# A fixed table for the ends of blocks in a four-layer sparse graph attention kernel: 18 finer steps, each half moved by itself

## The chip, the core and the metric

The kernel runs on one core of one Trainium2 chip. The metric is the device time of one execution in microseconds (us), lower is better. Three runs of the kernel before took 2247.27, 2250.97 and 2253.18 us; their median is 2250.97 us.

A core has engines that each run their own instructions in order: TensorE (PE, matrix products; its weight loads are shown apart as PEld), VectorE (DVE), ScalarE (ACT) and GpSimd (POOL). SP is the queue from which plain transfers (DMA) are issued; indirect gathers are issued by POOL.

## The reference

A batch of 16 graphs shares one adjacency matrix of 1024 nodes (about 8 neighbours a node). Four layers follow each other; layers 0, 2 and 3 are attention layers, layer 1 is a graph attention layer of one head.

```python
Q, K, V = (h @ Wq), (h @ Wk), (h @ Wv)            # 8 heads of 16
scores = einsum('bnhd,bmhd->bhnm', Q, K) / sqrt(16)
attn = softmax(where(adj == 0, -inf, scores))      # over the neighbours
x = layer_norm(h + einsum(attn, V) @ Wo + bo)
y = relu(x @ W1 + b1) @ W2 + b2                    # 128 -> 256 -> 128
x = layer_norm(x + y)
# layer 1: z = x @ W; scores = leaky_relu(z @ a_src + (z @ a_dst)^T), masked, softmax;
#          x = layer_norm(attn @ z + x)
```

Everything is in 32-bit floats[...].

## The kernel before, in words

**Tiling.** The 16 graphs are cut into two groups `g` of 8. The nodes are sorted by degree and dealt into 8 blocks `t` of 128. A *block* (called unit `u` in the code) is one layer, one group, 128 nodes: 16 blocks to a layer, 64 in all. The neighbours of a block are fetched from a table of keys and values in HBM, by indirect gathers; each block has some 4 to 6 *parts* of two gathered neighbours a partition (usually five: P0, P1, P2, then MIX, a part of one neighbour, then P4).

**One iteration of the main loop is one part** (lines 1160 to 1219). For an attention block DVE multiplies the gathered keys with the queries (`products`, L958), sums over the head dimension (L981), ACT takes the exponential (L985), DVE multiplies the gathered values with it one iteration later (`weighted`, L1009), and PE adds the rows up with a 0/1 matrix into PSUM (`summed`, `acc`, L1025). Products live in four buffers `pr`; a fifth one waits until PE has summed the oldest. P0 and P1 are summed together, in the iteration of MIX. POOL then issues the gathers of the part four ahead into the buffer that was just read.

**The end of a block.** When all parts are summed, the reciprocal of the denominators is taken (`divided`, L1062), and two *halves* of four graphs each (`h` = 0 and 1, here a and b) get their tile `o` (L1065) and a generator `attention_tail` (L703). The tail does everything else of the layer: transpose of `o` and the bias on the residual (L712, L717), Wo (L721, L722), layer norm (`normed`: squares L624, reciprocal root L630 and L631, scaling L639), transpose (L727), W1 and relu (L732, L741), W2 (L746, L750), layer norm, transpose, and the keys and values for the next layer's table (`project`, L576, L580, L585). In the last layer there are output transposes and an indirect store instead.

**What sets the order.** All engines follow the order of the program (`manual_schedule`). Each iteration has three *openings*, calls of `others()`: opening A after `summed`, before L981 and the exponential; opening B after the exponential, before L1009; opening C at the end of the iteration. A tail is a chain of steps (`yield`), 13 for half a; half b starts one step later. At an opening the pace is added up, and each time it reaches 1, `advance(tails)` moves both halves by one step. The pace is even: `(STEPS - LATE)` = 12 or 11 steps over the 14 openings after the first. So the last one or two steps of a block fall into the next. Every opening also takes one step of the side work: the query generator of the next block (`queries`, L880: for each half a projection and copy, L900 and L904, and then four repetitions over partitions with four copies, L909 and L912), loads, and in layer 0 the slow making of the second group's table. The first opening of a block's tail is opening C of the next block's second part; A, B and C of the parts P2, MIX and P4 follow, then A, B and C of the first part and A and B of the second part of the block after: 15 openings where a block has five parts.

**Buffers that the steps touch.** `banks`: four PSUM banks for all passing products (the four repetitions of a half of the queries take all four). `ybanks`: two. `hidden()`, the tile of relu outputs `f1`: one, shared by both halves. `o`, `oT`: two each.

Of the kernel before, what the change touches and what calls it, by code (L numbers as in the profile page):

```python
# [137 lines left out]
def sparse_path(ctx: ExitStack, tc: tile.TileContext, a: dict, out: bass.AP, flag):  # L138
# [474 lines left out]
    def normed(y, dve=False):  # L613

        z = twos.tile([P, GH, D], F32, tag="o", name="z")
        total = smalls.tile([P, GH], F32, tag="total", name="total")
        if dve:
            nc.vector.tensor_copy(z, y)
            nc.vector.tensor_tensor(z, z, y, ALU.mult)
            nc.vector.tensor_reduce(total, z, mybir.AxisListType.X, ALU.add)  # L620
            nc.vector.tensor_scalar(total, total, 1.0 / D, EPS, ALU.mult, ALU.add)
        else:
            for i in range(GH):
                nc.scalar.activation(  # L624
                    z[:, i, :], y[:, i, :], AF.Square, scale=D**-0.5, bias=root,
                    accum_out=total[:, i : i + 1],
                )
        yield
        rstd = smalls.tile([P, GH], F32, tag="rstd", name="rstd")
        nc.scalar.activation(rstd, total, AF.Ln)  # L630
        nc.scalar.activation(rstd, rstd, AF.Exp, scale=-0.5)  # L631
        if dve:
            nc.vector.tensor_tensor(
                z, y,
                rstd.rearrange("p (g o) -> p g o", o=1).to_broadcast([P, GH, D]), ALU.mult,
            )
            return z
        for i in range(GH):
            nc.scalar.activation(z[:, i, :], y[:, i, :], AF.Copy, scale=rstd[:, i : i + 1])  # L639
        return z  # L640
# [62 lines left out]
    def attention_tail(l, g, t, h, o):  # L703
        layer = LAYERS[l][0]
        p = {n: w[layer, n] for n in ATTN if (layer, n) in w}
        xt = xs[l, g, t][:, h]
        last = (l, g, t) == units[-1]
        dve = last and h > 0
        for _ in range(0 if last else h):
            yield  # L710
        oT = twos.tile([P, GH, P], F32, tag="oT", name="oT")
        turned(o, oT, dve=dve)  # L712

        if dve:
            nc.vector.tensor_scalar(xt, xt, p["bo"], None, ALU.add)
        else:
            nc.scalar.activation(xt, xt, AF.Identity, bias=p["bo"])  # L717
        yield
        ps = ybanks.tile([P, GH, D], F32, tag="yps", name="yps")
        for i in range(GH):  # L720
            nc.tensor.matmul(ps[:, i, :], oT[:, i, :], p["Wo"], start=True, stop=False)  # L721
            nc.tensor.matmul(ps[:, i, :], xt[:, i, :], centre, start=False, stop=True)  # L722
        yield
        z = yield from normed(ps, dve)
        yield
        x1 = twos.tile([P, GH, P], F32, tag="oT", name="x1")
        turned(z, x1, p["ln1_g"], p["ln1_b"], dve)  # L727
        yield
        f1 = (queries_of_shared if dve else hidden)().rearrange("p (f c) -> p f c", f=F)
        for f in range(F):  # L730
            ps = bank([P, GH * P])
            nc.tensor.matmul(  # L732
                ps, p["W1"][:, f * P : (f + 1) * P], x1.rearrange("p g n -> p (g n)"),
                start=True, stop=True,
            )
            if dve:
                nc.vector.tensor_scalar(
                    f1[:, f, :], ps, p["b1"][:, f : f + 1], 0.0, ALU.add, ALU.max
                )
            else:  # L740
                nc.scalar.activation(f1[:, f, :], ps, AF.Relu, bias=p["b1"][:, f : f + 1])  # L741
        yield
        ps = ybanks.tile([P, GH, D], F32, tag="yps", name="yps")
        for i in range(GH):
            for f in range(F):
                nc.tensor.matmul(  # L746
                    ps[:, i, :], f1[:, f, i * P : (i + 1) * P], p["W2"][:, f, :],
                    start=(f == 0), stop=False,
                )
            nc.tensor.matmul(ps[:, i, :], x1[:, i, :], centre, start=False, stop=True)  # L750
        yield
        z = yield from normed(ps, dve)
        yield
        yield from finish(l, g, t, h, z, p["ln2_g"], p["ln2_b"], dve)
# [55 lines left out]
    def at_once(g):  # L810
# [12 lines left out]
        for t in range(T):  # L823
# [9 lines left out]
            while both:  # L833
                advance(both)
                yield

    def exponents():
        return exps.tile([P, MOST * G * H], F32, tag="ex", name="ex")

# [40 lines left out]
    def queries(u):  # L880

        l, g, t = units[u]
        if not is_attention(u):
            ps = bank([P, J + 1, G])
            for j in range(J):
                nc.tensor.matmul(ps[:, j, :], rep_of(j, True), srcs[g, t], start=True, stop=True)
            for s, (j, _) in enumerate(QUARTERS[t]):
                at = slice(32 * s, 32 * s + 32)
                nc.tensor.matmul(
                    ps[at, MIX, :], rep_of(j, True)[:, at], srcs[g, t], start=True, stop=True  # L890
                )
            ofs[u] = smalls.tile([P, J + 1, G], F32, tag="of", name="of")
            nc.scalar.copy(ofs[u], ps)
            return
        qs[u] = reps.tile([P, J, ROW], F32, tag="qr", name="qr")
        for h in range(HF):
            q = ones_.tile([P, GH * D], F32, tag="q", name="q")
            ps = bank([P, GH, D])
            for i in range(GH):
                nc.tensor.matmul(  # L900
                    ps[:, i, :], xs[l, g, t][:, h, i, :], w[LAYERS[l][0], "Wq"],
                    start=True, stop=True,
                )
            nc.scalar.copy(q, ps.rearrange("p g d -> p (g d)"))  # L904
            yield
            pss = []
            for j in range(J):
                ps = bank([P, GH * D])
                nc.tensor.matmul(ps, rep_of(j), q[32 * j : 32 * j + 32], start=True, stop=True)  # L909
                pss.append(ps)  # L910
            for j in range(J):
                nc.scalar.copy(qs[u][:, j, h * GH * D : (h + 1) * GH * D], pss[j])  # L912
            yield

    def shared(u):

# [136 lines left out]
    def divided(u):  # L1053

        l, g, t = units[u]
        heads, d = (H, HD) if is_attention(u) else (1, D)
        den = bank([P, G * heads])
        for n, c in enumerate(sum(PIECES[t], [])):
            marked(t, c, den, exs[u][:, n, :])
        both = smalls.tile([P, 2, G * heads], F32, tag="both", name="both")  # L1060
        yield
        nc.vector.reciprocal(both[:, 1, :], den)  # L1062
        for h in range(HF):
            o = twos.tile([P, GH, D], F32, tag="o", name="o")
            nc.vector.tensor_tensor(  # L1065
                o.rearrange("p g (a d) -> p (g a) d", d=d),
                accums[u][:, h, :].rearrange("p (a d) -> p a d", d=d),
                both[:, 1, h * GH * heads : (h + 1) * GH * heads]
                .rearrange("p (a o) -> p a o", o=1)
                .to_broadcast([P, GH * heads, d]),  # L1070
                ALU.mult,
            )
            tails.append((attention_tail if heads > 1 else graph_tail)(l, g, t, h, o))
        nc.scalar.copy(both[:, 0, :], den)
        yield
        n = G * heads
        nc.gpsimd.tensor_tensor(seen[:, :, :n], seen[:, :, :n], both, ALU.add)
# [14 lines left out]
                free.append(gen)  # L1092

    pace = [0.0, 0.0]

    def idle():
        return slow if held[0] or not busy[0] else []

    def others():
        pace[0] += pace[1]  # L1100
        while pace[0] >= 1.0:
            advance(tails)
            pace[0] -= 1.0
        while True:
            gens = fronts or loads or idle()
            if not gens:
# [5 lines left out]
            if got == "idle":  # L1112
                advance(idle())
            break
        for _ in range(eager[0]):
            advance(idle())

    eager = [1]

    with tc.manual_schedule():  # L1120
# [39 lines left out]
        for i in range(len(parts) + 2):  # L1160
# [45 lines left out]
                    pass  # L1206
            if closing is not None and here:
                while any(gen not in free for gen in tails):
                    advance(tails)
                next(closing)  # L1210
                sizes, closing = closing, None
                passes = 3 if is_attention(u) else 4
                steps = STEPS if is_attention(done) else GRAPH_STEPS
                steps -= LATE[units[done][0]]
                pace[:] = 0.0, steps / (passes * sum(part[0] == u for part in parts) - 1)
            others()
            if i + 1 >= len(parts) or parts[i + 1][0] != u:

                while fronts:
                    advance(fronts)  # L1220
        while tails:
            advance(tails)
        for _ in closing:
# [438 lines left out]
```

## Time and profile before

| what | value |
|---|---|
| median of three runs | 2250.97 us |
| profiled execution | 2254.23 us, span 2251.9 us, TensorE clock granted 0.962 |
| PE busy | 2043.1 us, 91% |
| DVE busy | 1872.9 us, 83% |
| ACT busy | 1528.3 us, 68% |
| POOL busy | 1016.3 us, 45% |
| DMA | 636.05 MB, mean 282 GB/s |

The busy time is a union of the engine's intervals in the span. The mean of one instruction in a group is its latency, which for pipelined matmuls is longer than the distance between two of them; where the text needs a price it uses the distance in the timeline. Waits are inferred from semaphores: a row says which engine and line stood idle, for whom, how long in all, how often, and the longest.

### The profile page before, as it was taken

Reading aid. Unit: us, or ns where it says so; the run is one execution under the profiler, and the core shown is the slowest. Engines: PE = TensorE matmul, PEld = TensorE weight load, DVE = VectorE, ACT = ScalarE, POOL = GpSimd, SP = SyncE. Lnnn points to the kernel's source line nnn. Section 1 sums busy time; section 2 is a strip of 40 time slices with the busy share of each in tenths; the row PEclk is TensorE's granted clock in tenths of the full one; section 3 lists DMA queues with packets and bytes.
Section 4 is the critical chain, followed back from the end, with each engine's and each line's share of the span. In section 5 each row is a group of like instructions: output and inputs, shape, how many; then the busy total and the mean of one; then the engine's idle time right before and its main releaser. Section 6 shows DMA issues by size and latency. Waiting matters only on the chain.

```text
span 2251.9 us, 36507 instructions
## 1 busy us (share of the span) xinstructions
PE 2043.1 (91%) x13140; PEld 1271.3 (56%) x13140; DVE 1872.9 (83%) x1472; ACT 1528.3 (68%) x5041; POOL 1016.3 (45%) x699
## 2 busy tenths in 40 slices
PE   6589999899999999998999989999999998998986
PEld 5456665555555555554556655656655555555554
DVE  7897899888887577768988889989798998888893
ACT  3346777777777655555677777777777777676765
POOL 3343445354435368884343434334444544453540
PEclk8799999999999999999999999999999998999999
DMA  7897877778788699997997978887888788687860
GB/s 254 290 323 275 298 272 279 268 263 289 284 296 272 221 341 356 360 358 291 327 329 268 318 260 302 303 313 276 284 282 305 265 286 279 225 279 271 288 227 21
DMA packets 164700, 636.05 MB, mean 282 GB/s; under 512 B 34568, under 2 KB 37384, under 8 KB 116014
## 3 DMA queue, kind: packets, MB, share of 16 engines
q0 software_dynamic: 88720, 485.08, 61.0%
q1 hardware_dynamic: 75792, 148.57, 19.1%
q8 instruction: 105, 1.72, 0.3%
q14 instruction: 83, 0.68, 0.1%
HBM read 581.08 MB, written 92.34 MB: 299 GB/s over the span
## 4 chain that ended last, share of the span: by engine, by line
PE 41%; ACT 18%; issue 16%; DVE 11%; DMA 9%; POOL 5%; POOLq 0%; DVEq 0%; ACTq 0%
PE acc L1025 9%; DMA e<-table,idx 8%; PE yps L746 5%; PE ps L576 4%; POOL e L946 4%; PE ps L646 4%; ACT qr L912 4%; PE ps L732 3%; PE ps L909 3%; DVE pr L958 3%; ACT z L624 3%; DVE sc L981 3%; DVE pr L1009 2%; PE yps L750 2%; ACT z L639 2%
## 5 line engine op out<-in xcount | busy, mean ns | idle before, releaser
L946 POOL DMA_INDIRECT e<-table,idx x576 | 854.1, 1483 | 1101.8 <-DVE pr L1009 902.1
L1009 DVE TENSOR_TENSOR pr<-e,ex 128x2048 f32<-128x2048 f32 (+1 forms) x320 | 661.6, 2076 | 46.7 <-ACT ex L985 24.9
L958 DVE TENSOR_TENSOR pr<-e,qr 128x2048 f32<-128x2048 f32 x192 | 441.6, 2300 | 132.7 <-PE acc L1025 55.7
L1025 PE MATMUL acc<-pr,marks 128*32 128x512 f32 x2624 | 519.1, 608 | 14.8 <-DVE pr L1009 10.8
L981 DVE TENSOR_REDUCE sc<-pr 128x128 f32<-128x2048 f32 (+1 forms) x240 | 497.5, 2073 | 8.0
L624 ACT ACTIVATE z<-yps,root 128x128 f32<-128x128 f32 x888 | 317.5, 388 | 35.7 <-PE yps L765 17.2
L1025 PEld LDWEIGHTS acc<-pr,marks 128*32 128x32 f32 x2624 | 107.7, 110 | 269.4 <-issue 226.7
L639 ACT ACTIVATE z<-yps,rstd 128x128 f32<-128x128 f32 x888 | 254.0, 369 | 7.2
L746 PE MATMUL yps<-W,f 128*128 128x128 f32 x1520 | 251.8, 283 | 7.3 <-ACT f L741 1.8
L741 ACT ACTIVATE f<-ps,b 128x512 f32<-128x512 f32 x190 | 129.8, 695 | 157.6 <-PE ps L732 157.2
L746 PEld LDWEIGHTS yps<-W,f 128*128 128x128 f32 x1520 | 205.0, 192 | 51.0 <-issue 25.6
L576 PE MATMUL ps<-Wkv,xT 128*128 128x256 f32 x768 | 215.0, 419 | 20.0 <-ACT xT L652 16.7
L912 ACT COPY qr<-ps 128x512 f32<-128x512 f32 x384 | 197.3, 600 | 40.6 <-PE ps L909 40.5
L909 PE MATMUL ps<-q,rep 32*128 32x512 f32 x768 | 175.3, 661 | 34.7 <-ACT q L904 33.5
L732 PE MATMUL ps<-x,W 128*128 128x512 f32 x384 | 190.4, 620 | 12.5 <-ACT x L654 12.5
L624 ACT ACTIVATION_READ_ACCUMULATOR z<-yps,root 128x1 f32 x888 | 201.7, 227 | 0.0
L646 PE MATMUL ps<-ident,z 128*128 128x128 f32 x896 | 177.5, 299 | 25.5 <-ACT z L639 20.7
L646 PEld LDWEIGHTS ps<-ident,z 128*128 128x128 f32 x896 | 115.2, 142 | 149.2 <-ACT z L639 72.1
L580 ACT COPY kv<-ps 128x512 f32<-128x512 f32 x176 | 103.2, 589 | 131.9 <-PE ps L576 119.4
L576 PEld LDWEIGHTS ps<-Wkv,xT 128*128 128x128 f32 x768 | 146.5, 205 | 76.4 <-ACT xT L652 21.1
L721 PE MATMUL yps<-Wo,oT 128*128 128x128 f32 x768 | 160.3, 292 | 8.6 <-ACT oT L652 8.5
L722 PE MATMUL yps<-centre,x 128*128 128x128 f32 x768 | 155.5, 285 | 3.6
(176 smaller groups left out, 2597.7 us busy)
## 6 DMA issues: line engine op xcount, KB each, us to landing
table<-kv SPq DMA_DIRECT2D x88, 512.0 KB, 6.5
kept<-xT SPq DMA_DIRECT2D x96, 256.0 KB, 5.4
x<-kept SPq DMA_DIRECT2D x48, 512.0 KB, 9.2
qx<-qr SPq DMA_DIRECT2D x48, 256.0 KB, 6.7
e<-table,idx POOLq DMA_INDIRECT x576, 8.1
table<-kv SPq DMA_DIRECT2D x32, 256.0 KB, 7.7
qx<-qr SPq DMA_DIRECT2D x18, 384.0 KB, 9.1
qx<-qr SPq DMA_DIRECT2D x42, 128.0 KB, 8.1
```

The source lines that it names most:

```text
L576: nc.tensor.matmul(ps[:, k, :], x[:, i + k, :], w[LAYERS[l][0], "Wkv"], start=True, stop=True,)
L624: nc.scalar.activation(z[:, i, :], y[:, i, :], AF.Square, scale=D**-0.5, bias=root, accum_out=total[:, i : i + 1],)
L639: nc.scalar.activation(z[:, i, :], y[:, i, :], AF.Copy, scale=rstd[:, i : i + 1])
L646: nc.tensor.transpose(ps[:, i, :], z[:, i, :], ident)
L732: nc.tensor.matmul(ps, p["W1"][:, f * P : (f + 1) * P], x1.rearrange("p g n -> p (g n)"), start=True, stop=True,)
L746: nc.tensor.matmul(ps[:, i, :], f1[:, f, i * P : (i + 1) * P], p["W2"][:, f, :], start=(f == 0), stop=False,)
L912: nc.scalar.copy(qs[u][:, j, h * GH * D : (h + 1) * GH * D], pss[j])
L946: nc.gpsimd.indirect_dma_start(out=es[i][:, k, :], out_offset=None, in_=tables[l, g][:, :], in_offset=bass.IndirectOffsetOnAxis(ap=idx[:, ...
L958: nc.vector.tensor_tensor(prs[i][0][:, :n, :], es[i][:, :n, :ROW], qx[u].rearrange("p (o c) -> p o c", o=1) if (MIX, 0) in piece else of_p ...
L981: nc.vector.tensor_reduce(sc[:, :n, :], prs[i][0][:, :n, :].rearrange("p k (a d) -> p k a d", d=HD), mybir.AxisListType.X, ALU.add,)
L1009: nc.vector.tensor_tensor(prs[i][k0 // 2][:, :m, :].rearrange("p k (a d) -> p k a d", d=d), es[i][:, k0 : k0 + m, base : base + ROW].rearr ...
L1025: nc.tensor.matmul(outs[32 * j : 32 * j + 32], marks[:, mark, :], rhss, start=(chunk == mine[0]), stop=(chunk == mine[-1]),)
```

## The change

1. **Finer steps.** A tail has 18 steps instead of 13. `normed` yields once more, between the reciprocal root and the scaling (twice a tail); the transpose of `o` and the bias are two steps; the two halves of W1 and relu are two; W2 is two steps of two graphs. In order: 1 transpose of `o`, 2 bias, 3 Wo, 4 squares, 5 root, 6 scaling, 7 transpose, 8 and 9 W1 and relu, 10 and 11 W2, 12 squares, 13 root, 14 scaling, 15 transpose, 16 to 18 keys and values of the next layer.
2. **A table instead of the pace.** `PLAN` has one string for each of 15 openings. An `a` moves half a by one step, `b` half b, `q` takes one step of the side work. The strings hold 18 a, 18 b and 15 q. Beyond the table an opening does `abq`. The initial wait of half b (one step) is gone. The table drives the tails of attention blocks; those of layer 1 keep the pace.
3. **Queries in smaller pieces.** The repetitions of one half are two steps: the four products with the first two copies, and the last two copies. A query generator has six steps instead of four.
4. At the end of a block the drain of unfinished tails goes through the table too, and so does the rest after the last part.

```diff
+    PLAN = (
+        "aaqbabaqqb", "aqa", "qb", "a", "bbaabaqb", "abqq", "a", "baaqbb", "qqa", "", "bqqbqaaab", "", "", "q", "bbb",
+    )
@@ normed
         nc.scalar.activation(rstd, rstd, AF.Exp, scale=-0.5)
+        yield
@@ attention_tail
-        for _ in range(0 if last else h):
-            yield
         oT = twos.tile([P, GH, P], F32, tag="oT", name="oT")
         turned(o, oT, dve=dve)
-
+        yield
         if dve:
...
                 nc.scalar.activation(f1[:, f, :], ps, AF.Relu, bias=p["b1"][:, f : f + 1])
-        yield
+            yield
...
             nc.tensor.matmul(ps[:, i, :], x1[:, i, :], centre, start=False, stop=True)
-        yield
+            if i % 2:
+                yield
@@ queries
                 nc.scalar.copy(qs[u][:, j, h * GH * D : (h + 1) * GH * D], pss[j])
-            yield
+                if j % 2:
+                    yield
@@ the openings
+    def planned(beyond="abq"):
+        n = opening[0]
+        opening[0] += 1
+        for c in PLAN[n] if n < len(PLAN) else beyond:
+            if c == "q":
+                aside()
+                continue
+            for gen in tails:
+                if half_of[gen] == "ab".index(c):
+                    step(gen, tails)
+                    break
...
     def others():
+        if opening[0] is not None:
+            planned()
+            for _ in range(eager[0]):
+                advance(idle())
+            return
         pace[0] += pace[1]
         while pace[0] >= 1.0:
             advance(tails)
             pace[0] -= 1.0
+        aside()
...
                 while any(gen not in free for gen in tails):
-                    advance(tails)
+                    if opening[0] is None:
+                        advance(tails)
+                    else:
+                        planned("ab")
...
+                opening[0] = 0 if is_attention(done) else None
```

More of the change, by code (lines that the diff above doesn't have):

```diff
@@ L1073, in divided @@
             tails.append((attention_tail if heads > 1 else graph_tail)(l, g, t, h, o))
+            half_of[tails[-1]] = h
         nc.scalar.copy(both[:, 0, :], den)
@@ L1094, in sparse_path, with step @@
     pace = [0.0, 0.0]
+    opening = [None]
+    half_of = {}
+    def step(gen, gens):
+        got = next(gen, "end")
+        if got == "end":
+            gens.remove(gen)
+        elif got == "free":
+            free.append(gen)
+    def planned(beyond="abq"):
[9 more added lines that the diff above has]
+                    break
     def idle():
@@ L1103, in others, with aside @@
             pace[0] -= 1.0
+        aside()
+        for _ in range(eager[0]):
+            advance(idle())
+    def aside():
         while True:
@@ L1114, in others @@
             break
-        for _ in range(eager[0]):
-            advance(idle())
     eager = [1]
@@ L1215, in sparse_path @@
                 pace[:] = 0.0, steps / (passes * sum(part[0] == u for part in parts) - 1)
+                if is_attention(done) and opening[0] is None:
+                    for gen in list(tails):
+                        if gen in free:
+                            for _ in gen:
+                                pass
+                            tails.remove(gen)
+                opening[0] = 0 if is_attention(done) else None
             others()
@@ L1220, in sparse_path @@
                     advance(fronts)
+        while opening[0] < len(PLAN):
+            planned()
         while tails:
```

## The prediction

> **What bounds the kernel now.** I read the page first, then the busy time of one steady block, then who waits for whom in a steady stretch (1100 to 1640 us, most of layer 2), then that stretch in order of time.
>
> The page's busy line, and from the table of stretches one block of layer 2 (length, then PE, weight loads, DVE, ACT, POOL busy):
>
> ```profile
> PE 2043.1 (91%) x13140; PEld 1271.3 (56%) x13140; DVE 1872.9 (83%) x1472; ACT 1528.3 (68%) x5041; POOL 1016.3 (45%) x699
> ...
> 1524.00:1560.00 36.00, 34.32 (x224) 21.67 (x223) 32.13 (x19) 27.52 (x88) 14.18 (x10) 1.00 0.91 319
> ```
>
> In 36 us PE is busy 34.3, DVE 32.1, ACT 27.5. No engine is full; nothing has more than 9 us to give. The reciprocal L1062 marks the blocks: its starts in DVE's timeline lie 550.1 us apart over the 15 intervals of layer 2 and 540.8 over those of layer 3, 36.4 us a block. DVE's own work in a block, by the distances in its timeline (2.32 + 2.2 + 2.2 a part, 3.5 for MIX, 1.9 for reciprocal and the two `o`) is 4 x 6.72 + 3.5 + 1.9 = 32.3. So 4.1 us a block are waits of DVE. Which ones, by the view of waits of DVE from 1100 to 1640 us (total, times, longest; 14.8 blocks):
>
> ```profile
> DVE pr L958 <- PE acc L1025: 21.7, 12, 4.0
> DVE pr L958 <- DMA e<-table,idx: 19.2, 8, 5.5
> DVE pr L1009 <- ACT ex L985: 6.6, 4, 3.5
> DVE both L1062 <- PE ps L1025: 5.5, 3, 2.7
> ```
>
> A block loses 1.5 us to the product buffer that PE has not yet summed, 1.3 to a late gather, only 0.45 to a late exponential, 0.4 to the denominators. The first of them in order of time (start, length, engine):
>
> ```profile
> 1153.45 1.29 DVE L1065 TENSOR_TENSOR o<-acc,both 128x512 f32<-128x512 f32 x2
> ...
> 1163.76 2.28 DVE L1009 TENSOR_TENSOR pr<-e,ex 128x2048 f32<-128x2048 f32 x1
> 1170.09 2.29 DVE L958 TENSOR_TENSOR pr<-e,qr 128x2048 f32<-128x2048 f32 x1 [4.05 <-PE acc L1025]
> ```
>
> After `o`, DVE runs P2 and MIX without a stop and then needs the buffer of P0; PE frees it only here:
>
> ```profile
> 1164.35 1.86 PE L909 MATMUL ps<-q,rep 32*128 32x512 f32 x8
> ...
> 1168.13 1.92 PE L1025 MATMUL acc<-pr,marks 128*32 128x512 f32 x16
> ```
>
> And ACT at the same time, one queue in the order of the program, the exponential of MIX last:
>
> ```profile
> 1164.46 0.59 ACT L652 COPY oT<-ps 128x512 f32<-128x512 f32 x1 [1.63 <-PE ps L646]
> 1164.94 0.72 ACT L717 ACTIVATE x<-x,bo 128x512 f32<-128x512 f32 x1
> 1165.57 2.04 ACT L912 COPY qr<-ps 128x512 f32<-128x512 f32 x4
> 1167.46 0.41 ACT L624 ACTIVATE z<-yps,root 128x128 f32<-128x128 f32 x1
> ...
> 1168.85 0.31 ACT L985 ACTIVATE ex<-sc 128x64 f32<-128x64 f32 x1
> ```
>
> What is placed ahead of an exponential on ACT delays it; before the change little is, and MIX's exponential comes 15 us after `o` half a (1154.1).
>
> **What the skill says.** The Trainium skill, "PSUM — Partial Sum Buffer", section "Engine vs sequencer instructions", has ScalarE's and VectorE's queues as strict FIFO, and matmuls as starting and completing in program order. The trace agrees: L985 at 1168.85 follows exactly the copies and squares issued ahead of it. "Perfetto Trace Analysis", section "Optimization Strategy", says that the same bubble repeated can mean that no buffer is free for the next tile; the 1.5 us a block at L958 is such a one.
>
> **The change, part by part.** No arithmetic is added or removed: the same instructions in another order. A `yield` costs nothing on the chip. All is in what stands ahead of what.
>
> *Where the steps fall.* In layers 2 and 3 the old pace gives openings 1 to 3 of a block (counted from 0) the first three steps, the queries' rest and the old block's last steps, and opening 4 nothing. The table gives opening 0 a1 a2 q b1 a3 b2 a4 q q b3, opening 1 a5 q a6, 2 q b4, 3 a7, and opening 4 b5 b6 a8 a9 b7 a10 q b8. Openings 1, 4, 7 lie before the exponentials of P2, MIX, P4. Summing of P0 and P1 comes right before opening 4.
>
> *Ledger of ACT from `o` half a (time 0) to MIX's exponential.* Prices are distances in the timeline above and around it: copy 0.5 to 0.6, bias 0.7, four squares 1.4, root 0.45, scaling 1.1, four query copies 2.0, relu 0.7, transposed copy with gain 0.75, exponential 0.3. Opening 0: 0.5+0.7+0.6+0.5+0.7+1.4+2.0 = 6.4. Opening 1: 0.45+0.6+1.1, and the exponential of P2: 2.45. Openings 2 and 3: 1.0+1.4+0.75 = 3.15. Opening 4: 0.45+1.1+0.7+0.7+0.75+1.0+0.7 = 5.4. Together 17.4, plus what ACT must wait for: the first transpose 0.9; Wo of a 0.5; the second query projection 1.0 (queued behind b3 on PE); and the relu of b8. There is one `f1`: b8 writes it before a11, the last reader of a's, has been issued, so that relu waits for W2's second half on PE. With PE at 14.2 (below) and W1 of a twice 0.9, transpose 0.6, relus and half of W2 to 19, W1 of b 0.9, a11 1.3, it ends near 21.2: 2.0 us of wait. MIX's exponential ends at 17.4+0.9+0.5+1.0+2.0+0.3 = 22.1. Before it came at 15.
>
> *DVE in that time.* Rest of `o` 0.6, P2 with P1's weighting 6.7, MIX's two products 2.4: at 9.7 it wants the exponential of P2, which ACT has at 0.9+6.4+0.5+0.45+1.0+0.6+1.1+0.3 = 11.25: stall 1.55. Weighting to 13.5. Then P4 needs the sum of P0 and P1. PE: opening 0 0.1+0.6+1.1+0.6+2.0+1.8+2.0 = 8.2, projection 1.1, wait for its copy on ACT to 9.9, repetitions 1.8, transpose 0.6, sum 1.9: 14.2, stall 0.7. P4's two operations end at 18.7, and MIX's weighting waits to 22.1: stall 3.4. After it the table is thin (11 and 12 are empty, and the exponential of P4 is 0.3 late). Sum 32.3+1.55+0.7+3.4+0.3 = 38.25. The late gather (in these blocks the next P0's, 15 us from its weighting to landing at 1720 to 1735) gets over 16 us now and is hidden; that gain is in the sum.
>
> *What the hand count leaves out.* The same count for the old order gives 32.3 + 1.3 gather + 0.2 for `acc`, some 34 to 35, against 36.4 measured: hand-overs and bank waits of about 1.5. In the new order part of them disappear under the ACT queue. I take half, 0.75: 39.0, or 2.6 more a block. Ends for it: 0 and 1.5, so 1.85 to 3.4.
>
> *The rest.* The wait of PE for the query copy (`PE ps L909 <- ACT q L904`, 17.9 us in 14.8 blocks, 1.2 each) goes away for half a of the queries; PE then stands about 3 us at the transpose of `o` instead, which is at nothing because DVE sets the end there. If that cover were gone it would be worth up to 1.2. The last keys and values leave their block earlier, which nobody waits for: the table they fill is read 8 blocks later. The SP stores and POOL's `seen` move with them, ahead of no gather that is due. Layer 1 has one more step a tail; PE is busy 148.8 of 155 us there, the order hardly counts: bound 0 to 5 us, taken 0. The very end alternates the halves as before: -3 to 3, taken 0.
>
> *Sum.* Blocks with an attention block on both sides: 15 in layer 0, 15 in layer 2, one between layers 2 and 3, 15 in layer 3: 46. 46 x 2.6 = 120. The profiled execution of 2254.2 (span 2251.9 and 2.3 around it) becomes 2374; it lies 3.3 above the median, which becomes 2371.
>
> **Rivals.**
> *Faster.* The bubbles close: `acc` is on time (1.5 a block) and ACT keeps up. 46 x 1.5 = 69 less, 2182. It decides if MIX's exponential is done before 18.7, that is if ACT's ledger of 17.4 waited for under 1.3 us in all. For it: ACT is 24% idle, and PE's waits for ACT's copies are real. Against: 17.4 of the block's 27.5 us of ACT work stand in half of its time. Chance 0.10.
> *About the same, a little slower.* The relu of b8 waits 0, not 2, because PE is ahead: stalls 1.55+0.7+1.4+0.3, block 36.25 to 37.0, at most 46 x 0.6 = 28: 2245 to 2290. For it: the wait of b8 is nowhere in the old trace. Chance 0.16, a third of it within 0.3%.
> *Much slower.* Every hand-over counts in full and delays the next block's queries (last copy at 20 of the block, needed at 23) or the first layer's slow work: 41 a block, 46 x 4.6 = 212, 2463. Chance 0.10.
> The forecast: 0.64, its own range 2310 to 2440.
>
> **How the numbers follow.** 0.3% (7 us) is what a measurement of this kernel can tell from no change. Faster: the first rival, 0.10. Same 0.05. Slower 0.85. Cutting the faster rival, most of the much slower one and the bottom of the second leaves 2262 to 2445.
>
> **What would show it.** Right: DVE's waits for `ex` (L985) rise from 0.45 to about 5 us a block and are the largest row; the gather row nearly vanishes; blocks of 39 us; ACT f L741 waits for PE yps L746, which has no large row now; PE's share falls below 88%. Wrong: blocks under 36.4, or DVE's waits still led by `acc` and gathers. If `ex` is not late, the ledger is wrong; if ACT does not wait at b8, only its 2.0 is.

## The result and the profile after

The changed kernel takes 2380.18 us (median of 6 runs), the kernel before 2249.12 us on the same chips: a ratio of 1.0583, 95% interval 1.0553 to 1.0613, slower. The forecast was 2371, slower, range 2262 to 2445. The profiled execution is 2377.5 us, its span 2375.3.

The page of the changed kernel, its busy line, and from the table of stretches one block of layer 2 (from one reciprocal to the next):

```profile
PE 2004.4 (84%) x13140; PEld 1289.1 (54%) x13140; DVE 1875.7 (79%) x1472; ACT 1531.3 (64%) x5041; POOL 1037.2 (44%) x699
```

```profile
1567.60:1606.00 38.40, 33.61 (x220) 22.11 (x220) 32.35 (x20) 27.82 (x88) 15.16 (x10) 0.96 0.82 287
```

The work is the same, and the shares are lower because it stands in more time (the busy time of DVE and ACT is within 3 us of before, that of PE is 39 us less). DVE is busy 32.35 us of the block, against 32.13 in the block shown of the kernel before. What the block is longer, 2.4 us, is nearly all waits. The view of waits of DVE in layer 2 of the changed kernel (1141 to 1713 us; total, times, longest):

```profile
DVE pr L1014 <- ACT ex L990: 62.5, 36, 3.3
DVE pr L963 <- PE acc L1030: 10.1, 12, 1.4
DVE pr L963 <- ACT qr L916: 9.8, 2, 4.9
DVE pr L963 <- DMA qx<-qr: 4.0, 1, 4.0
```

(L963, L986, L990, L1014 are L958, L981, L985, L1009 of the kernel before.) The wait for the exponential (L990) has gone from the third row to the first; the gather's row is gone; `acc` has halved. In order of time, DVE in one block, the stalls alone:

```profile
1580.23 2.29 DVE L1014 TENSOR_TENSOR pr<-e,ex 128x2048 f32<-128x2048 f32 x1 [1.66 <-ACT ex L990]
1583.36 2.29 DVE L963 TENSOR_TENSOR pr<-e,qr 128x2048 f32<-128x2048 f32 x1 [0.83 <-PE acc L1030]
...
1590.45 1.23 DVE L1014 TENSOR_TENSOR pr<-e,ex 128x1024 f32<-128x1024 f32 x1 [2.48 <-ACT ex L990]
...
1597.06 2.29 DVE L1014 TENSOR_TENSOR pr<-e,ex 128x2048 f32<-128x2048 f32 x1 [0.86 <-ACT ex L990]
```

Four stalls: P2, the sum of P0 and P1, MIX, P4, 5.83 us together. The last three repeat almost to the hundredth from block to block (the next block has 1.46, 0.83, 2.49, 0.86). The first does not. Two other blocks of the same layer, in the view of stretches (its third number from the end is the granted clock of PE):

```profile
1528.02:1567.59 39.57, 34.67 (x220) 23.29 (x220) 32.36 (x20) 27.83 (x88) 15.15 (x10) 0.91 0.82 291
1644.19:1680.96 36.77, 32.09 (x226) 20.57 (x226) 32.35 (x19) 27.61 (x88) 18.05 (x10) 1.00 0.80 283
```

DVE and ACT are as busy in the one as in the other. In the first DVE waits 2.83 us for P2's exponential, in the second not at all. PE stands some 3 us before the transpose of `o` in both (3.13 and 3.02). After that its clock is 0.50 from 1529 to 1535 us in the first, and 1.00 in the second; one microsecond of each, with 7 and 12 matmul instructions:

```profile
1529.44 1.09 PE L647 MATMUL ps<-ident,o 128*128 128x128 f32 x4 [3.13 <-DVE o L1070]
1532.00:1533.00 1.00, 1.00 (x7) 1.00 (x6) 0.96 (x2) 0.58 (x1) 0.00 (x0) 0.50 1.00 395
1648.00:1649.00 1.00, 1.00 (x12) 1.00 (x11) 0.96 (x2) 1.00 (x2) 1.00 (x1) 1.00 1.10 363
```

So Wo comes later, and with it the squares on ACT and the exponential behind them. Nineteen blocks of five parts in layers 2 and 3 (left out are those next to a change of layer or behind a block of six parts, and one more with other work on DVE) fall in order: 36.8 us at a mean clock of 1.00 (four blocks), 38.1 to 38.4 at 0.95 to 0.96 (eight), 38.5 to 38.6 at 0.93 (three), 39.5 to 39.6 at 0.89 to 0.91 (four). In the kernel before no such order is seen; it has a block of 38.65 us at 1.00 and one of 35.62 at 0.90, and PE stands before `o` only three times in these two layers, 3.5 us in all.

And ACT ahead of MIX's exponential, with its wait for the single `f1`:

```profile
1586.82 1.06 ACT L916 COPY qr<-ps 128x512 f32<-128x512 f32 x2
1589.59 0.69 ACT L740 ACTIVATE f<-ps,b 128x512 f32<-128x512 f32 x1 [1.70 <-PE yps L745]
1590.17 0.25 ACT L990 ACTIVATE ex<-sc 128x64 f32<-128x64 f32 x1
```

`o` half a was ready at 1568.86 (L1070 from 1568.17, two of 0.69); MIX's exponential ends at 1590.42, 21.6 us later, where the ledger had 22.1.

Where the 123 us of the two spans lie, by the starts of the reciprocals number 1, 9, 16, 32, 40, 48, 56 and 64 in DVE's timeline; the last column runs from the last one to the end:

| us | start | layer 0, g 0 | layer 0, g 1 | layer 1 | layer 2, g 0 | layer 2, g 1 | layer 3, g 0 | layer 3, g 1 | end |
|---|---|---|---|---|---|---|---|---|---|
| before | 161.8 | 322.5 | 247.1 | 310.9 | 293.7 | 296.6 | 295.1 | 287.6 | 36.6 |
| changed | 164.6 | 353.4 | 266.2 | 317.3 | 301.0 | 310.6 | 313.6 | 307.1 | 41.6 |
| exponentials first | 160.5 | 318.9 | 230.1 | 312.9 | 281.2 | 283.2 | 290.8 | 279.7 | 40.5 |
| old pace, exponentials first | 166.0 | 340.2 | 266.3 | 310.6 | 299.0 | 295.6 | 292.8 | 286.2 | 38.5 |
| finer steps, old places | 162.2 | 346.1 | 228.7 | 332.0 | 280.1 | 282.7 | 294.6 | 291.3 | 48.0 |

### The profile page after: what moved, and what is told of

The parts are those of the page before. It is cut to its first block, busy times and chain, and to the rows that moved or that the text cites. A ratio compares the mean times of both kernels' runs of the same rounds, so it can differ in the third digit from the quotient of the medians.

```text
span 2375.3 us, 36561 instructions
## 1 busy us (share of the span) xinstructions
PE 2004.4 (84%) x13140; PEld 1289.1 (54%) x13140; DVE 1875.7 (79%) x1472; ACT 1531.3 (64%) x5041; POOL 1037.2 (44%) x699
## 4 chain that ended last, share of the span: by engine, by line
PE 48%; ACT 19%; DVE 17%; issue 11%; DMA 3%; POOL 2%; POOLq 0%; DVEq 0%; ACTq 0%
PE acc L1030 8%; PE yps L745 8%; ACT z L624 6%; PE ps L647 6%; DVE pr L1014 6%; PE ps L731 4%; DVE pr L963 4%; ACT z L640 4%; PE ps L904 4%; PE yps L720 4%; PE yps L721 4%; PE yps L749 4%; ACT qr L916 3%; PE ps L913 3%; PE ps L576 2%
## 5 line engine op out<-in xcount | busy, mean ns | idle before, releaser
L951 POOL DMA_INDIRECT e<-table,idx x576 | 922.4, 1601 | 1180.6 <-DVE pr L1014 950.3
L1014 DVE TENSOR_TENSOR pr<-e,ex 128x2048 f32<-128x2048 f32 (+1 forms) x320 | 660.8, 2074 | 268.8 <-ACT ex L990 243.6
L986 DVE TENSOR_REDUCE sc<-pr 128x128 f32<-128x2048 f32 (+1 forms) x240 | 497.5, 2073 | 8.1
L963 DVE TENSOR_TENSOR pr<-e,qr 128x2048 f32<-128x2048 f32 x192 | 438.8, 2286 | 69.9 <-PE acc L1030 35.3
L1030 PEld LDWEIGHTS acc<-pr,marks 128*32 128x32 f32 x2624 | 108.0, 111 | 290.8 <-issue 237.2
L745 PE MATMUL yps<-W,f 128*128 128x128 f32 x1520 | 243.0, 281 | 2.5 <-ACT f L740 1.5
L647 PE MATMUL ps<-ident,o 128*128 128x128 f32 x384 | 85.9, 367 | 171.4 <-DVE o L1070 167.3
L576 PE MATMUL ps<-Wkv,xT 128*128 128x256 f32 x768 | 204.7, 407 | 20.5 <-ACT xT L653 16.4
L916 ACT COPY qr<-ps 128x512 f32<-128x512 f32 x384 | 202.5, 604 | 13.1 <-PE ps L913 12.9
L740 ACT ACTIVATE f<-ps,b 128x512 f32<-128x512 f32 x190 | 131.0, 692 | 115.9 <-PE yps L745 82.4
L647 PE MATMUL ps<-ident,z 128*128 128x128 f32 x896 | 159.5, 291 | 47.3 <-ACT qr L916 22.3
L624 ACT ACTIVATION_READ_ACCUMULATOR z<-yps,root 128x1 f32 x888 | 188.4, 212 | 0.0
L647 PEld LDWEIGHTS ps<-ident,z 128*128 128x128 f32 x896 | 106.9, 142 | 144.4 <-ACT qr L916 50.4
L990 ACT ACTIVATE ex<-sc 128x128 f32<-128x128 f32 (+1 forms) x240 | 73.2, 307 | 165.7 <-DVE sc L986 165.6
L647 PEld LDWEIGHTS ps<-ident,o 128*128 128x128 f32 x384 | 63.1, 192 | 191.7 <-issue 136.9
```

The costliest lines, as they stand in the source:

```text
L576: nc.tensor.matmul(ps[:, k, :], x[:, i + k, :], w[LAYERS[l][0], "Wkv"], start=True, stop=True,)
L624: nc.scalar.activation(z[:, i, :], y[:, i, :], AF.Square, scale=D**-0.5, bias=root, accum_out=total[:, i : i + 1],)
L647: nc.tensor.transpose(ps[:, i, :], z[:, i, :], ident)
L745: nc.tensor.matmul(ps[:, i, :], f1[:, f, i * P : (i + 1) * P], p["W2"][:, f, :], start=(f == 0), stop=False,)
L951: nc.gpsimd.indirect_dma_start(out=es[i][:, k, :], out_offset=None, in_=tables[l, g][:, :], in_offset=bass.IndirectOffsetOnAxis(ap=idx[:, ...
L963: nc.vector.tensor_tensor(prs[i][0][:, :n, :], es[i][:, :n, :ROW], qx[u].rearrange("p (o c) -> p o c", o=1) if (MIX, 0) in piece else of_p ...
```

## The experiments

Two theories stood at the start. **Q**: the loss is the queue; exponentials stand behind tail steps on ACT. **P**: the loss is PE's, which now stands for long before the transpose of `o` and whose granted clock has fallen from 0.962 to 0.936. Their rows in the waits of the whole run of the changed kernel:

```profile
DVE pr L1014 <- ACT ex L990: 243.6, 122, 6.6
PE ps L647 <- DVE o L1070: 167.3, 40, 7.3
```

### Exponentials first

```diff
+            if here and opening[0] is not None:
+                exponentials(i)
+            planned_here = opening[0] is not None
             others()
-            if here:
+            if here and not planned_here:
                 exponentials(i)
```

> The changed kernel, but while the table is in force the sum over heads and the exponential of a part are issued before opening A instead of after it; table, steps and queries stay. Theory Q (the loss is the exponential standing behind tail steps in ScalarE's queue): the row of VectorE's waits for ex, 243.6 us, falls below 40; products then wait more for acc (2 us a block, since PE is not faster) and for gathers (1 us); blocks of 36 to 36.5 instead of 38.5; time 2240 to 2300. Theory P (the loss is PE's: it stands 167 us before the transpose of o and its granted clock is 0.936 instead of 0.962): time stays within 2360 to 2400.

Measured: 2200.98 us, ratio to the kernel before 0.9788 (0.9762 to 0.9813). That is 179 us under the changed kernel and below what theory Q allowed. Waits of DVE in the whole run:

```profile
DVE pr L963 <- PE acc L1030: 64.9, 35, 9.1
...
DVE pr L1014 <- ACT ex L990: 8.7, 7, 3.4
```

The row of 243.6 us is 8.7 now. PE's wait for `o` fell by itself, from 167.3 to 52.6 us, and its clock stands at 0.965. So Q names the start of the loss, and PE's standing is an effect of it. It is an effect with a price of its own, though: by the blocks above, the low clock that follows it makes P2's exponential later still. This run takes both away at once, and none takes away only one. The kernel beats both others: with the exponentials (and the sums over heads, which move with them) out of the way, the new order as a whole is a gain.

### Is it the exponential's place alone?

The same move in the kernel before, with its even pace:

```diff
+            early = here and is_attention(u)
+            if early:
+                exponentials(i)
             others()
-            if here:
+            if here and not early:
                 exponentials(i)
```

> The kernel before (old pace, coarse steps), with the sum over heads and the exponential of every attention part issued before opening A. Theory Q: before the change exponentials were hardly late (waits for ex 0.45 us a block in layer 2), so little is to be had: 0 to 30 us less, time 2220 to 2255; the table is then what makes the kernel with exponentials first fast. Rival G (moving the exponential is a gain of its own, table or not): time below 2215.

Measured: 2298.49 us, 1.0176 (1.0133 to 1.0218): slower, outside both expectations. The table of stretches says where: layers 2 and 3 are within 6 us of before, as Q has it; layer 0 alone loses 37 us, with `acc` the largest wait of DVE there (48.8 us against 20.7). ACT's and PE's timelines of layer 0 show what stands in the way: an exponential that is not ready yet. In one block ACT waits 1.24 us at it for DVE's sum (311.19 us), copies the transposed `o` after it (311.76), and PE waits 1.75 us for that copy before Wo. These waits of PE for `oT` are 24.3 us in layer 0, against 3.7 in the kernel before. Whether they account for all 37 was not tested. So the exponential's place is worth nothing by itself; it is worth 179 us to this table, which put much in front of it.

### Fineness, by itself

A first try laid the finer letters evenly over openings 1 to 14:

```diff
     PLAN = (
-        "aaqbabaqqb", "aqa", "qb", "a", "bbaabaqb", "abqq", "a", "baaqbb", "qqa", "", "bqqbqaaab", "", "", "q", "bbb",
+        "qq", "aaq", "abbqq", "abq", "aab", "abbq", "aab", "aabbq", "abbq", "aabq", "abb", "abq", "ab", "abq", "bq",
```

> The changed kernel with another table: the same 18 finer steps, halves moved apart and query pieces, but the letters are laid out as the old even pace had them (half b one old step behind half a, one to three old steps an opening over openings 1 to 14). Theory Q: only the places count, not the fineness; ex waits below 60 us, blocks of 36 to 37, time 2225 to 2285. Rival F (more steps, halves by themselves or query pieces cost by themselves): time above 2330.

Measured: 2430.73 us, 1.0796 (1.0768 to 1.0824), far outside. It was no faithful copy: the old pace, in layers 2 and 3, leaves two steps of half a and three of half b to the next block and so comes to half b's W1 after P4's exponential, this table before it. DVE and ACT in one of its blocks:

```profile
1595.06 2.29 DVE L1014 TENSOR_TENSOR pr<-e,ex 128x2048 f32<-128x2048 f32 x1 [4.07 <-ACT ex L990]
```

```profile
1593.29 0.69 ACT L740 ACTIVATE f<-ps,b 128x512 f32<-128x512 f32 x1 [4.69 <-PE ps L731]
1594.14 0.69 ACT L740 ACTIVATE f<-ps,b 128x512 f32<-128x512 f32 x1 [0.17 <-PE ps L731]
1594.73 0.30 ACT L990 ACTIVATE ex<-sc 128x128 f32<-128x128 f32 x1
```

Same illness, other place: one relu that waits 4.69 us for PE holds the exponential behind it. A second wait came with it, the reciprocal for PE (129.0 us in the run). Next a table that is faithful to layers 2 and 3 (layer 0's old pace had one step more inside the block); capital letters step a half's old generator only, if there is one:

```diff
+        "qq", "ABaaq", "ABabbqq", "Babq", "q", "aabq", "abbq", "aabq", "aabbq", "q", "abbq", "aabq", "abb", "abq", "q",
...
+            mine = [gen for gen in tails if half_of[gen] == "ab".index(c.lower())]
+            if c in "ab" and mine:
+                step(mine[-1], tails)
+            elif len(mine) > 1:
+                step(mine[0], tails)
```

> The changed kernel with the 18 finer steps, but a table that puts every old step into the opening where the old pace had it in layers 2 and 3, with the last steps of each half left for openings 1 to 3 of the next block, and with the exponential where the change has it. If fineness and the table as such cost nothing: 2235 to 2265. Rival F (more steps or query pieces cost by themselves): above 2290.

Measured: 2267.19 us, 1.0040 (1.0025 to 1.0055), just above the upper end expected for "fineness costs nothing", by 2 us, and far from the rival. By the stretches it gains in the second group of layer 0 and in layer 2 (18 and 28 us) and loses in the first group of layer 0 and in layer 1 (24 and 21). So 18 steps, moved by a table, cost next to nothing as a whole, by gains and losses that cancel; by the ratios to the kernel before, 0.054 of the change's 0.058 come from where the table puts them. In layer 2 this kernel is as fast as the one with exponentials first (280.1 and 282.7 us against 281.2 and 283.2), so what that one gains there over the kernel before does not need the new places. Elsewhere it is behind it: 27 us in the first group of layer 0, 19 in layer 1, 15 in layer 3. Why it gains in layer 2 was not tested.

### Which late exponential counts

One letter, half b's first W1 and relu, moved behind the last reader of `f1`:

```diff
-        ... "bbaabaqb", "abqq",
+        ... "bbaabaq", "abbqq",
```

> The changed kernel with one letter moved: the eighth step of half b (first W1 and relu) goes from the end of opening 4 to behind a11 in opening 5. Theory Q with its term for the single f1 buffer: the row ACT f <- PE yps (82 us) vanishes, the exponential of MIX comes 2.5 us earlier, its stall of 2.5 us a block goes, of which 0.5 may come back at P4: 46 x 1.8 to 2.5, time 2265 to 2300. Rival (f1 is not on the path, the queue ahead of it is full anyway): 2360 to 2385.

Measured: 2375.91 us, 1.0563 (1.0533 to 1.0594): nothing; the rival's number. DVE's timeline of one block of this run, and ACT's two relus of half b:

```profile
1585.92 1.22 DVE L1014 TENSOR_TENSOR pr<-e,ex 128x1024 f32<-128x1024 f32 x1
...
1594.90 2.29 DVE L1014 TENSOR_TENSOR pr<-e,ex 128x2048 f32<-128x2048 f32 x1 [3.24 <-ACT ex L990]
```

```profile
1587.59 0.69 ACT L740 ACTIVATE f<-ps,b 128x512 f32<-128x512 f32 x1 [1.71 <-PE ps L731]
1588.45 0.69 ACT L740 ACTIVATE f<-ps,b 128x512 f32<-128x512 f32 x1 [0.17 <-PE ps L731]
```

The row ACT f <- PE yps is gone and MIX's stall of 2.48 is gone with it. But ACT's wait is not gone. It has moved behind MIX's exponential and changed its name: 1.70 us for W2 is now 1.71 for W1, because PE does half b's W1 behind half a's W2. P4's stall has grown from 0.86 to 3.24. Half b's second relu starts 21.75 us after `o` half a in both kernels (1590.61 - 1568.86 and 1588.45 - 1566.70), each time just released by PE, and P4's weighting starts 28.2 us after it in both (1597.06 - 1568.86 and 1594.90 - 1566.70). The row through ACT and PE to P4's exponential has the same length whichever relu comes first. A second `f1` was not tried; judged from these lines, PE's order would hold the second relu all the same. Then the opposite move, P4's exponential alone:

```diff
+            early = here and opening[0] == 7 and i == begun + 4
+            if early:
+                exponentials(i)
             others()
-            if here:
+            if here and not early:
                 exponentials(i)
```

> The changed kernel with one exponential only moved ahead of its opening, that of the fifth part (P4), in front of opening 7. Theory C (the exponentials are late one after the other in one ScalarE chain; only the last of them sets the end of the block, the stalls at P2 and MIX are slack in front of it): the stall of 0.86 us at P4 goes and nothing else changes, 46 x 0.86 = 40 us less, time 2330 to 2350. Rival S (the stalls add up, each with its own price): the same 40 at most; so the run is read with the one that took MIX's stall away and gained nothing: under S that one should have gained 90. If this run gains nothing either, both fall and the queue of tail steps alone, wherever the exponential stands, sets the block.

Measured: 2337.56 us, 1.0353 (1.0303 to 1.0403), 42.6 less than the changed kernel (52 by the ratios to the kernel before, 37 between the profiled executions) against 40 worked out. Most of its five-part blocks repeat at 37.4 and 37.5 us at a clock of 0.95, with 1.66, 0.83 or 0.84 and 2.48 still there at P2, the sum and MIX: 0.8 less on average than the changed kernel's at 0.95 to 0.96. The one at a clock of 1.00 takes 35.8 against 36.8. By the stretches the gain is uneven, 26 us in layer 0, 5 in layer 2, 15 in layer 3, and a loss of 7 in layer 1; in layer 2 this run has one of its usual blocks at 1.00 where the changed kernel has four. Together the two runs show it: a stall of 2.48 us that went away in the middle gained nothing, 0.86 taken away at the end gained about itself in blocks of the same clock.

### The queries

The sixth q, the last two query copies, moved from opening 4 to 2:

```diff
-        ... "aqa", "qb", "a", "bbaabaqb",
+        ... "aqa", "qqb", "a", "bbaabab",
```

> The changed kernel with one letter moved: the sixth q (last two query copies) goes from opening 4 to opening 2. In blocks of four parts the next block's P0 follows right after MIX, and the six waits of products for the query copies, 4.9 to 6.8 us each, 31.7 us in all, vanish. Theory: 25 to 35 us less, time 2343 to 2357. Rival (the wait turns into one for the exponential at the same place): 2370 to 2385.

Measured: 2410.69 us, 1.0712 (1.0688 to 1.0735): 30 us more instead of 30 less. The waits at four-part blocks did fall (31.7 to 13.5 us), but other blocks grew, those of five parts in layer 2 by 0.9 us on average. One of them in DVE's timeline:

```profile
1605.53 1.23 DVE L1014 TENSOR_TENSOR pr<-e,ex 128x1024 f32<-128x1024 f32 x1 [3.46 <-ACT ex L990]
```

MIX's stall is 3.46 instead of 2.48, for the 1.06 us of the two copies. In the changed kernel they stand right before the relu that waits 1.70 us for PE, and so cost nothing; earlier they push everything behind them, PE's work for that relu included (it waits 2.84 us in this block). Undoing the third part of the change, whole queries, puts more there:

```diff
             for j in range(J):
                 nc.scalar.copy(qs[u][:, j, h * GH * D : (h + 1) * GH * D], pss[j])
-                if j % 2:
-                    yield
+            yield
```

> The changed kernel with the third part of the change undone: the repetitions of a half of the queries and their four copies are one step again, so that the queries are done in opening 1. The two copies that fell into ScalarE's wait at opening 4 then stand before the exponential of P2: 1 us a block more as with the early q, less the waits at four-part blocks: 2390 to 2415. Rival (query pieces are what makes the change slow): below 2365.

Measured: 2518.12 us, 1.1170 (1.1127 to 1.1212), more than 100 us over what was expected. The reason is in ACT's timeline in opening 1 of a block:

```profile
1613.39 2.05 ACT L916 COPY qr<-ps 128x512 f32<-128x512 f32 x4 [1.80 <-PE ps L913]
1615.30 1.18 ACT L640 ACTIVATE z<-yps,rstd 128x128 f32<-128x128 f32 x4
1616.31 0.36 ACT L989 ACTIVATE ex<-sc 128x128 f32<-128x128 f32 x1
```

With whole queries the fourth q is the second half's repetition itself: 2.05 us of copies and 1.80 of waiting for PE in front of P2's exponential, whose stall grows from 1.66 to between 5.2 and 6.5. Only the copies' length had been counted, not the wait of the first of them. MIX's and P4's stalls stay at 2.4 and 0.87, so the whole chain is that much longer. The query pieces are a repair that this table needs, not a cost.

With exponentials first, the early q was tried again, then with the `f1` letter as well:

```diff
-        ... "aqa", "qb", "a", "bbaabaqb", "abqq",
+        ... "aqa", "qqb", "a", "bbaabab", "abqq",     (first)
+        ... "aqa", "qqb", "a", "bbaaba", "abbqq",     (second)
```

> The changed kernel with exponentials first and also the sixth q in opening 2 instead of 4. In the run with opening A after the exponential removed as a delay, ScalarE's tail work no longer stands before an exponential, so the 1 us a block that the early query cost should be gone and its gain of up to 32 us at the ends of four-part blocks stay: 2170 to 2190. Rival (the copies delay the next transposes and W1 on PE as well): 2200 or more.

> As the last one, and the first W1 of half b moved behind a11 as well. If the single f1 buffer still costs ScalarE its 1.7 us a block when exponentials are out of its way, DVE's waits for acc fall and it is faster than the last one by 5 to 30 us; if ScalarE has room, they are the same within 5 us.

Measured: 2249.75 us, 0.9961 (0.9948 to 0.9974), and 2251.65 us, 0.9982 (0.9966 to 0.9997). The rival's side: 39 us more than with exponentials first alone, by the ratios. Between the profiled executions it is 46, and 28 of it lie in layer 0, where a q also steps input loads. The two are the same within 2 us: moving that relu is worth nothing there either. Last, the early q only where the block has four parts:

```diff
+        letters = PLAN[n] if n < len(PLAN) else beyond
+        if small[0]:
+            letters = {2: "qqb", 4: "bbaabab"}.get(n, letters)
```

> The changed kernel with exponentials first (as the first run, 2201 us), and the sixth q in opening 2 only where the block has four parts. There products wait 5.0 to 6.8 us for the query copies at the next block's P0, six times, 32.4 us in that run; everywhere else the early q cost time. If that wait is on the path: 2168 to 2185. If what follows it (the copy qx, the sum of P0 and P1) was as late anyway: 2192 to 2205.

Measured: 2202.95 us, 0.9770 (0.9721 to 0.9820): no gain over 0.9788 that these runs can tell. The wait for the query copies fell from 32.4 to 12.1 us and the sum stayed. What was late behind it is late still: DVE's waits for the denominators went from 34.8 to 42.1 us, those for `acc` from 64.9 to 67.3. Why the early q costs what it does in layer 0 stays open.

## Why the prediction was right

**The place and the kind were right.** The busy time of DVE and ACT did not move, the exponential became the first wait (4.2 us a block in layer 2, where about 5 stood), the gather was hidden, PE fell below 88%, ACT's relu waited for PE yps (82.4 us, 43 times, 1.9 each, where the ledger had 2.0).

**The ledger, term by term**, for the block at a clock of 0.96 and for the one at 1.00:

| stall in a block | worked out | measured, 0.96 | measured, 1.00 |
|---|---|---|---|
| P2's exponential | 1.55 | 1.66 | none |
| sum of P0 and P1 | 0.7 | 0.83 | 0.83 |
| MIX's exponential | 3.4 | 2.48 | 2.48 |
| P4's exponential | 0.3 | 0.86 | 0.86 |
| all | 5.95 | 5.83 | 4.17 |

That the first row fits is luck. ACT's waits up to P2's exponential were put at 2.4 us (0.9, 0.5 and 1.0). At the full clock they are 1.3 (0.82, 0.34, 0.17); in the block of the first column 2.7 (0.88, 0.51, 0.27, 0.92, 0.16), and what they have more comes with PE's slow stretch, which the ledger does not have.

**PE standing before `o`, priced at nothing, was not rightly so.** The prediction saw the 3 us of standing come and gave as its reason that DVE sets the end there. PE stood 167 us in all, 3 us a block in most of layer 2 and 5 in most of layer 3, and often ran at half its clock after it. The blocks that escaped this take 36.8 us, 0.4 more than the 36.4 before; the mean is 38.2. So by the blocks of this trace about 1.4 of the 1.8 us that a block has lost come with the low clock. That is an estimate from blocks alike in DVE's and ACT's busy time and in the stalls behind P2, not an experiment. The queue stays the start of it: when the exponentials were moved, 115 us of the standing went and the clock came back.

**The allowance was too much.** The hand count gave 38.25 us a block and 0.75 was added for hand-overs. From the first to the last reciprocal of layer 2 it is 572.3 us over 15, and of layer 3 572.5 over 15: 38.2 a block, 1.8 more than before and not 2.6. That 38.2 meets 38.25 says little, since it is an average over clocks.

**The total came right in part by other terms.** The 31 blocks from layer 2 on gave 60 us where 81 stood. Layer 0 grew by 50 us from reciprocal 1 to 16, 3.3 a block, where 39 stood. Start, layer 1 and end gave 13 more where 0 stood. Four-part blocks were not looked at: there P0 of the next block comes where P4 would and needs the copies of the sixth q, which ACT reaches late (one such copy starts at 1700.05 us, with DVE standing since 1695.75); products wait 4.9 us and more, six times, 31.7 us.

**One step was wrong in kind.** More than half of MIX's stall was priced as the wait for the single `f1`, and the second rival took it off the total at its full size. The wait is there, but with the relu behind the last reader of `f1` ACT waits as long for W1, and the time is the same (2375.91 us): the row's end counts. For the same reason "MIX's exponential before 18.7" was the wrong mark for the faster rival. Its mechanism was real: with ACT's tail work out of the exponential's way the table is faster than the kernel before, 0.9788.

## What to carry to other kernels

In an engine that keeps the order of the program, the price of a piece of work is what stands behind it and when that is due; count the queue from the last hand-over to each due point, its waits for other engines included, and follow the one that ends last. A stall at a due point in the middle of such a row can be slack: before paying for its removal, look whether the last one grows by the same. What lengthens the row itself is no slack, wherever it stands: whole queries in front of P2's exponential made every due point behind it late. A wait that changes its name has not gone. Time in which another engine stands can have its price later, as it had here in the clock; compare like blocks of one trace before putting it at nothing. And when a new order loses, ask first which small, urgent instruction it buried; moving that one forward may leave the order's gain standing.

## What the runs showed of the hardware that was not expected

In the changed kernel PE stands about 3 us before the transpose of `o`, and in most blocks its granted clock is 0.50 for some time after it: from 1529 to 1535 us in one block, from 1570 to 1572 in the next, not at all in a third. The starts of Wo's pairs of instructions lie 0.43 us apart at 0.50 and 0.22 at 1.00. Stands of 3.02 and 3.13 us occur with the drop and without it, so the length of the stand alone does not decide it; what does was not set apart.

Over a whole execution the mean clock is 0.962 before (PE busy 91%), 0.965 with exponentials first (88%), 0.963 with the early q besides (87%), but 0.939 with P4's exponential first (86%), 0.953 with the even table (85%), 0.936 in the changed kernel (84%) and 0.914 with whole queries (83%). It does not follow the busy share alone.
